# Window attention: the output projection's second block, the transposes' copies and the last projection piece placed differently

## The chip, the cores and the metric

The kernel runs on one core of one Trainium2 chip, in float32. The metric is the device time of one launch in microseconds. Before the change it is 5811.65 us, the median of three runs (5798.19 to 5814.1).

## The reference

The input x has shape (8, 56, 56, 192). Four layers follow one another; each normalises its input in groups and adds its result to it: two token-mixing layers with Toeplitz convolutions, a 7x7 depthwise convolution with an MLP, and a shifted-window attention. The change is in the last one, which computes this:

```python
x = jnp.roll(x, (-DISP, -DISP), (1, 2))       # DISP = 3, windows of WS*WS = 49
q, k, v = x @ Wq, x @ Wk, x @ Wv              # reshaped to (b, 6, nw, 49, 32)
scores = jnp.einsum('bhnqd,bhnkd->bhnqk', q, k) * DIM_V ** 0.5 + bias
...
attn = jax.nn.softmax(scores, axis=-1)
out = jnp.einsum('bhnqk,bhnkd->bhnqd', attn, v).reshape(b, n_h, n_w, -1)
out = jnp.roll(out @ Wfc + bfc, (DISP, DISP), (1, 2))
```

The reshape to (b, 6, nw, 49, 32) is one of memory order, without a transposition: a head is a stretch of rows, and its windows are runs of 49 times 32 numbers in it. Rows of the mask are added to some of the windows.

## The kernel before

The first three layers end at about 4900 us of the span; the attention takes the rest. It is one generator, `attention`, whose first steps are woven into the end of the MLP. The loop at its end, `for n in range(len(units) + 1)`, is what the change touches.

**Units, groups, slots.** A unit is half of one sample's rows, so there are 16, and one more turn of the loop that finishes the last. A unit's 48 windows per quarter are worked off in NG = 3 groups (`g` = 0, 1, 2; "first", "middle", "third" below). A group has four slots, `give(0)` to `give(3)`, at which pieces of other work are issued between the softmax's own. `order[g][slot]` lists them: 0 is a piece of the next unit's projection, 1 a block of the previous unit's output projection.

**Projection of the next unit** (`project`): ten pieces. Four value pieces (matmuls of L1176 and L1186, a copy on ScalarE, stores to a DRAM buffer and reloads by SP in another layout), then six query and key pieces (L1229), each with two copies into the tile `f`: one on VectorE (L1244) and one on ScalarE (L1242). The first group issues the four value pieces, the middle group two query pieces (slots 0 and 3), the third group the other four, the last of them in slot 3. The first scores of the next unit read what that last piece's copies write.

**Output projection of the previous unit** (`out`): two blocks. Block k0 covers 128 of the 192 output channels (48 matmuls, L1345), block k1 the remaining 64 (96 smaller ones). A block takes two PSUM tiles, and eight additions on VectorE (L1356) bring its result into the raw tiles `ra` (k0) or `rb` (k1). After k1, SP stores both to the output (L1366). k0 is issued in slot 1 of the middle group and k1 in slot 2. At the end of that group SP reloads the same two tiles (three buffers each) with the input of unit n+2 (L1133, L1135), and at the end of the third group `normalize` (L1151 on VectorE, L1159 on ScalarE) turns them into `xa` and `xb`, which have one buffer each and feed the next projection.

**Softmax.** In slot 0 and slot 1 of each group: `scores` (64 matmuls, L1259; on VectorE scaling with bias, L1271, and the maximum, L1280; on GpSimd the subtraction, L1281; on ScalarE the exponential, L1282), then after the slot's pieces `divide` (on VectorE the sum, L1289, and the reciprocal, L1290; on GpSimd the product, L1291). What a group has computed is used one group later: `turned` transposes it on TensorE (eight matmuls, L1297) and copies it from PSUM into `et`, for slot 0 by VectorE (L1307) and for slot 1 by ScalarE (L1305). `weighted` multiplies it with the values (64 matmuls, L1319), slot 0's ahead of `give(2)`, slot 1's after it, and `sixths` copies the result out (L1329 on VectorE, L1334 on ScalarE).

**PSUM** is one pool of four tiles, each two banks: `self.bank2 = lambda: ps.tile([128, 2, 512], F32, name="bank2")` with `bufs=4`. A piece of the projection, scores, transposes and a weighted sum take one tile each, a block of the output projection two.

**Order on the engines.** Each engine works off its own instructions in a fixed order, set when the program is built. It follows the order of the code, except that an instruction that can start sooner may stand ahead of another engine's result: in the trace the copy of L1307 runs between L1289 and L1290 in the middle and third groups, and the additions of k0 run behind the second sum, although the code has them ahead of it. On TensorE the order in the loop is that of the code.

Of the kernel before, what the change touches and what calls it, by code (L numbers as in the profile page):

```python
# [43 lines left out]
class Net:  # L44
# [1013 lines left out]
    def attention(self, L, xs, gn3, gnd, ys, vd):  # L1058
# [14 lines left out]
        if True:  # L1073
# [4 lines left out]
            def load_gr(i):  # L1078
                for half in HALF:
                    nc.sync.dma_start(gr[i][half], gnd[i].rearrange("(b c) s -> c b s", c=C)[128:C])  # L1080
# [169 lines left out]
            def scores(hh, g, i, qf, kf):  # L1250


                s = bank2()
                for n in range(8):
                    for half in range(2):
                        for c in range(2):
                            qd = slice(32 * (i + 2 * c), 32 * (i + 2 * c) + 32)
                            u = (16 * g + 8 * half + n) * WR
                            nc.tensor.matmul(  # L1259
                                s[64 * half : 64 * half + 64, c, n * WR : (n + 1) * WR],  # L1260
                                qf[qd, u : u + 64],
                                kf[qd, u : u + WR],
                                start=True,
                                stop=True,
                            )
                var = {0: 1, 3: 2}.get((2 * i + 3 * hh + g) % 4, 0)
                e = ering[count[0] % NE]
                count[0] += 1
                ev = e[:, :, :, :WR]
                e3 = e.rearrange("p c n k -> p (c n) k")[:, :, :WR]  # L1270
                nc.vector.scalar_tensor_tensor(  # L1271
                    ev,
                    view(s, 0, [[512, 2], [WR, 8], [1, WR]]),
                    math.sqrt(32.0),
                    view(bias, var * 8 * WR, [[0, 2], [WR, 8], [1, WR]]),
                    ALU.mult,
                    ALU.add,
                )
                mx = p.tile([128, 16], F32, name="mx", bufs=6)
                nc.vector.tensor_reduce(mx, e3, AX.X, ALU.max)  # L1280
                nc.gpsimd.tensor_sub(e3, e3, view(mx, 0, [[1, 16], [0, WR]]))  # L1281
                nc.scalar.activation(e3, e3, AF.Exp)  # L1282
                return e

            def divide(e):

                e3 = e.rearrange("p c n k -> p (c n) k")[:, :, :WR]
                sm = p.tile([128, 16], F32, name="sm", bufs=6)
                nc.vector.tensor_reduce(sm, e3, AX.X, ALU.add)  # L1289
                nc.vector.reciprocal(sm, sm)  # L1290
                nc.gpsimd.tensor_mul(e3, e3, view(sm, 0, [[1, 16], [0, WR]]))  # L1291

            def turned(e, i):
                pt = bank2()
                for c in range(2):
                    for m in range(4):
                        nc.tensor.transpose(  # L1297
                            pt[:113, c, m * 128 : m * 128 + 113],
                            e.rearrange("p c n k -> p c (n k)")[:113, c, m * 128 : m * 128 + 113],
                            self.ident[:113, :113],  # L1300
                        )
                et = self.at2.tile([113, 8, 113], F32, name="et", bufs=3)
                ev = pt.rearrange("p c (m q) -> p (c m) q", q=128)[:113, :, :113]
                if i:
                    nc.scalar.copy(et, ev)  # L1305
                else:
                    nc.vector.tensor_copy(et, ev)  # L1307
                return et
# [29 lines left out]
            def out(b, hh, ra, rb, oj):  # L1338
                for k, raw, n in ((0, ra, 7), (1, rb, 4)):
                    fs = [bank2(), bank2()]  # L1340
                    for j in range(6):
                        for i in range(4):
                            qd = slice(32 * i, 32 * i + 32)
                            for h in range(k + 1):
                                nc.tensor.matmul(  # L1345
                                    fs[i // 2][HALF[h] if k else slice(0, 128), i % 2, : n * W],
                                    wfc[qd, j, 128 * k : 128 * k + 128 - 64 * k],
                                    oj[qd, j, h * MT : h * MT + n * W],
                                    start=j == 0,
                                    stop=j == 5,  # L1350
                                )
                    for i in range(4):

                        for c, m, c2 in ((0, 53, 3), (53, 3, 0)):
                            to = raw[:, i, :, c2 : c2 + m]
                            nc.vector.scalar_tensor_tensor(  # L1356
                                to,
                                view(fs[i // 2], i % 2 * 512 + c, [[W, n], [1, m]]),
                                bfc[:, k : k + 1],
                                to,  # L1360
                                ALU.add,
                                ALU.add,
                            )
                    if k == 0:
                        yield
                rows(b, hh, ra, rb, (ys, lambda t, d: nc.sync.dma_start(d, t)), 1)  # L1366

            def step(gen):

                try:  # L1370
                    next(gen)
                except StopIteration as end:
                    return end.value
                return None
# [20 lines left out]
            late = None  # L1395


            order = (((0,), (0,), (0,), (0,)), ((0,), (1,), (1,), (0,)), ((0,), (0,), (0,), (0,)))
            for n in range(len(units) + 1):
                if n < len(units):  # L1400
                    (b, hh), (v, qf, kf) = units[n], now
                gen = project(*units[n + 1]) if n + 1 < len(units) else None
                outs = None
                now = None
                for g in range(NG):
                    if g == 1 and n:
                        outs = out(*units[n - 1], *raws.pop(n - 1), oj)

                    def give(at):
                        got = now  # L1410
                        for kind in order[g][at]:
                            if kind and outs is not None:
                                step(outs)
                            elif not kind and gen is not None:
                                got = step(gen)
                        return got

                    es, ets = [], []
                    for i in range(2):
                        if n < len(units):  # L1420
                            es.append(scores(hh, g, i, qf, kf))
                        now = give(i)
                        self.norm_part()
                        if n < len(units):
                            divide(es[i])
                        if late is not None:
                            ets.append(turned(late[1][i], i))
                    if late is not None:
                        g_late, es_late, v_late = late
                        if g_late == 0:  # L1430
                            ot = self.at2.tile([128, HR], F32, name="ot", bufs=1)
                            oj = self.at2.tile([128, 6, HT], F32, name="oj", bufs=1)
                        po = bank2()
                        weighted(g_late, 0, ets[0], v_late, po)
                    now = give(2)
                    if late is not None:
                        weighted(g_late, 1, ets[1], v_late, po)
                        sixths(g_late, po, ot, oj)
                    now = give(3)
                    late = (g, es, v) if es else None  # L1440
                    if g == 0 and n + 3 == len(units) // 2:
                        for more in self.all_norms():
                            pass
                        load_gr(1)
                    if g == 1 and n + 2 < len(units):
                        raws[n + 2] = load(*units[n + 2])
                    if g == 2 and n + 2 < len(units):
                        normalize(units[n + 2][0], *raws[n + 2])
# [197 lines left out]
```

## Time and profile before

| | |
|---|---|
| median of three runs | 5811.65 us |
| the profiled execution | 5810.6 us |
| its span, first to last instruction | 5808.7 us |
| mean granted TensorE clock | 0.957 |
| TensorE busy in the span | 5366.0 us (92%) |
| VectorE, ScalarE, GpSimd busy | 2367.7, 2262.1, 2205.1 us (41, 39, 38%) |
| attention loop, units 1 to 14 | 4951.82 to 5748.13 us |
| TensorE, VectorE busy in it | 715.51, 468.16 us of 796.31 |
| DMA engines in it, mean | 43%, 88 GB/s |

How it is read: a group of instructions is named by its line, engine and tiles. A wait is the idle time of an engine just before an instruction, put down to what released it; only waits of the engine that sets the pace cost time. "issue" is idle time for which the profile shows no releaser. The granted clock is the share of TensorE's full speed that the throttle allowed in a stretch. Matmuls overlap, so what one set of them costs is read from the start of one to the start of the next.

### The profile page before, as it was taken

The numbers are of one execution on the slowest core, as the hardware profiler recorded it, in microseconds if no ns is written. First come the engines' busy times: TensorE is split into PE (matmuls) and PEld (weight loads), VectorE is DVE, ScalarE is ACT, GpSimd is POOL, SyncE is SP. The second block draws the span as 40 slices with busy tenths as digits, with TensorE's granted clock in tenths as the row PEclk, the third lists the DMA queues.
The fourth block names the chain that finished last, engine by engine and source line by source line (L and its number), as shares of the span: only waits on it lengthen the run. The fifth ranks groups of instructions, "written<-read, shape, count | busy, mean of one in ns | idle before, by whom it ended". The sixth has DMA issues, their size and how long they took to land.

```text
span 5808.7 us, 144259 instructions
## 1 busy us (share of the span) xinstructions
PE 5366.0 (92%) x64672; PEld 3891.7 (67%) x64672; DVE 2367.7 (41%) x3770; ACT 2262.1 (39%) x2990; POOL 2205.1 (38%) x1528
## 2 busy tenths in 40 slices
PE   6998887999999999998888889989999999889898
PEld 3776665777777777776666678856664445666666
DVE  6444544233553333552333322332213232565655
ACT  2434444443554444554444322242323333333332
POOL 2335566564665566565566200000001001333333
PEclk9999998999999999999999899999999999999998
DMA  8559997888886887878998566634444223344442
GB/s 277 137 151 263 273 291 210 266 253 231 239 257 200 243 249 252 238 233 225 293 307 268 169 216 223 217 117 159 148 160 117 67 62 58 80 95 85 90 87 62
DMA packets 1029770, 1098.79 MB, mean 189 GB/s; under 512 B 232768, under 2 KB 966976, under 8 KB 1013728
## 3 DMA queue, kind: packets, MB, share of 16 engines
q1 hardware_dynamic: 993568, 888.57, 56.2%
q0 software_dynamic: 35584, 200.99, 9.0%
q8 instruction: 509, 8.34, 0.6%
q14 instruction: 109, 0.89, 0.0%
HBM read 725.48 MB, written 363.94 MB: 188 GB/s over the span
## 4 chain that ended last, share of the span: by engine, by line
PE 54%; POOL 7%; DMA 7%; SPq 6%; DVE 5%; issue 3%; ACT 3%; POOLq 0%; DVEq 0%; ACTq 0%
PE bank L263 8%; PE bank L955 6%; PE bank L816 5%; PE bank L1035 4%; PE bank L530 4%; PE bank L575 4%; SPq L392 3%; PE bank L405 3%; POOL s L427 3%; PE bank L1049 3%; DMA t<-L_sum 2%; SPq L379 2%; PE bank L539 2%; PE bank L1229 2%; DMA qv<-t 2%
## 5 line engine op out<-in xcount | busy, mean ns | idle before, releaser
L263 PE MATMUL bank<-wq,t 128*128 128x256 f32 (+4 forms) x7680 | 1300.3, 377 | 84.0 <-DVE t L272 46.2
L263 PEld LDWEIGHTS bank<-wq,t 128*128 128x128 f32 (+2 forms) x7680 | 1013.8, 192 | 364.7 <-issue 103.7
L272 DVE TENSOR_TENSOR t<-bank,wq 128x1024 f32<-128x1024 f32 (+3 forms) x480 | 517.7, 1112 | 773.7 <-PE bank L263 551.6
L304 POOL TENSOR_TENSOR t<-t 128x1024 f32<-128x1024 f32 (+2 forms) x288 | 518.9, 1815 | 654.3 <-ACT t L301 342.1
L412 ACT COPY ot<-bank 128x896 f32<-128x896 f32 x576 | 493.0, 914 | 631.3 <-PE bank L405 357.8
L427 POOL TENSOR_TENSOR s<-s,ot 128x1568 f32<-128x1568 f32 x144 | 618.6, 4300 | 68.7 <-DVE ot L425 68.2
L405 PE MATMUL bank<-q,tm 56*32 56x224 f32 x18432 | 522.2, 363 | 78.0 <-DMA tm<-L_tab 25.9
L301 ACT ACTIVATE t<-t 128x2048 f32<-128x2048 f32 (+2 forms) x288 | 422.0, 1488 | 397.2 <-DVE t L272 388.7
L405 PEld LDWEIGHTS bank<-q,tm 56*32 56x32 f32 x18432 | 351.1, 108 | 216.3 <-issue 108.5
L556 POOL TENSOR_TENSOR t<-t,t 128x896 f32<-128x896 f32 x168 | 347.2, 2085 | 362.8 <-DMA t<-L_sum 185.2
L588 DVE SCALAR_TENSOR_TENSOR t<-bank,wo,t 128x448 f32<-128x448 f32 x112 | 76.5, 683 | 889.9 <-ACT t L584 492.3
L530 PE MATMUL bank<-t,wo 128*128 128x224 f32 x1792 | 395.9, 377 | 45.5 <-ACT t L509 22.4
L955 PE MATMUL bank<-z,w 128*128 128x448 f32 (+1 forms) x1344 | 416.0, 557 | 3.1 <-ACT h L964 3.1
L549 ACT ACTIVATE t<-bank,wo 128x448 f32<-128x448 f32 x448 | 248.0, 635 | 406.7 <-PE bank L539 377.0
L530 PEld LDWEIGHTS bank<-t,wo 128*128 128x128 f32 x1792 | 351.7, 202 | 81.6 <-issue 30.8
L575 PE MATMUL bank<-t,wo 128*128 128x224 f32 x1792 | 378.9, 366 | 0.0
L127 POOL DMA_DIRECT2D x<-x x64 | 36.7, 573 | 865.4 <-DVE x L986 836.2
L575 PEld LDWEIGHTS bank<-t,wo 128*128 128x128 f32 x1792 | 338.0, 194 | 34.2 <-issue 32.4
L816 PEld LDWEIGHTS bank<-xt,cm 113*112 113x112 f32 x3072 | 315.0, 180 | 43.7 <-issue 38.3
L423 DVE STREAM_TRANSPOSE s<-ot 128x1792 f32<-128x1792 f32 x144 | 292.7, 2035 | 115.5 <-DMA L_sum<-s 86.6
L816 PE MATMUL bank<-xt,cm 113*112 113x108 f32 (+2 forms) x3072 | 326.2, 266 | 6.4 <-issue 3.3
L955 PEld LDWEIGHTS bank<-z,w 128*128 128x128 f32 (+1 forms) x1344 | 183.3, 190 | 208.2 <-issue 199.2
(149 smaller groups left out, 6996.6 us busy)
## 6 DMA issues: line engine op xcount, KB each, us to landing
q<-qv SPq DMA_DIRECT2D x36, 3584.0 KB
q<-qv SPq DMA_DIRECT2D x72, 1568.0 KB
L_sum<-s POOLq DMA_DIRECT2D x288, 392.0 KB, 7.7
t<-L_sum SPq DMA_DIRECT2D x112, 1008.0 KB
qv<-t SPq DMA_DIRECT2D x192, 512.0 KB
cm<-in_L_cm SPq DMA_DIRECT2D x96, 896.0 KB
tm<-L_tab SPq DMA_DIRECT2D x288, 240.0 KB
x<-t POOLq DMA_DIRECT2D x112, 336.0 KB, 7.1
```

Source lines behind the costliest of these rows:

```text
L263: nc.tensor.matmul(pp[:m, b, 256 * j : 256 * j + k], x[rows, j, 2 if part else b, s : s + m], w[rows, part, c0 + c : c0 + c + k],  start=p ...
L272: nc.vector.tensor_add(z[:m, c : c + k, :], view(pp[:m], 0, [[1, k], [256, 4]]), view(bias[:m], c0 + c, [[1, k], [0, 4]]),)
L301: nc.scalar.activation(z[:m, :n, :], z[:m, :n, :], AF.Silu)
L304: nc.gpsimd.tensor_mul(prod[:m, :k], half[:, :, 0], half[:, :, 1])
L405: nc.tensor.matmul(pt[32 * j : 32 * j + 32, r, hf * 224 : (hf + 1) * 224], tm[rows, at : at + 32], q[rows, :, 4 * c : 4 * c + 4], start=Tr ...
L412: nc.scalar.copy(view(ot, 4 * (g % 4), [[16, 2], [32, 112], [1, 4]]), view(pt, 0, [[512, 2], [4, 112], [1, 4]]),)
L427: nc.gpsimd.tensor_add(to, to, view(of, 0, [[1, 28], [32, 56]]))
L530: mm(gs[c // 2][:, b, c % 2 * 256 : c % 2 * 256 + N], pw[:, 0, 128 * c : 128 * c + 128], xn[:, b], start=c % 2 == 0, stop=False,)
L556: gate.tensor_mul(to, to, pg)
L575: mm(P[:, b, :N], ow[:, c, 0:128], g[:, 4 * b + c], start=False, stop=c == 3 and b == 1)
L816: nc.tensor.matmul(pc[:, 128 * e + 4 * m0 : 128 * e + 4 * m1], cm[:113, e, k, :], xt[:, m0 - 1 + k : m1 - 1 + k, c + e, :], start=n == 0 a ...
L955: nc.tensor.matmul(phs[c][:, s, :TT], w0[rows, part, at : at + 128], z[rows, Z[2 if part else s], :], start=part == flip, stop=part != flip,)
```

## The change

Three edits in `attention`, in 15 lines:

```diff
                 et = self.at2.tile([113, 8, 113], F32, name="et", bufs=3)
                 ev = pt.rearrange("p c (m q) -> p (c m) q", q=128)[:113, :, :113]
-                if i:
+                if i == 0:
                     nc.scalar.copy(et, ev)
                 else:
                     nc.vector.tensor_copy(et, ev)
...
-            order = (((0,), (0,), (0,), (0,)), ((0,), (1,), (1,), (0,)), ((0,), (0,), (0,), (0,)))
+            order = (((0,), (0,), (0,), (0,)), ((0,), (1, 0), (0,), (1,)), ((0,), (0,), (0,), ()))
...
                         now = give(i)
                         self.norm_part()
+                        if late is not None:
+                            ets.append(turned(late[1][i], i))
                         if n < len(units):
                             divide(es[i])
-                        if late is not None:
-                            ets.append(turned(late[1][i], i))
```

In the middle group, slot 1 now issues k0 and then a query piece, slot 2 a query piece, and slot 3 k1; so the middle group has three pieces of the projection instead of two. The third group has three instead of four, the last of them in slot 2, ahead of the second weighted sum; its slot 3 is empty. The stores of k1, which are issued with it, and the reload after it move with it on SP. Slot 0's transposes are copied by ScalarE and slot 1's by VectorE. In both slots the transposes and their copy are issued ahead of the division of the current group's scores.

## The prediction

> **What bounds the kernel now.** Only the attention loop is touched, so I read the granted clock first, then the busy time by stretch, TensorE's waits in the loop, and the instructions of one unit in order of time. The steady part is units 1 to 14: from the first scores of unit 1 (4951.82) to those of unit 15 (5748.13), 796.31 us or 56.88 a unit. What TensorE waited for there, in total, times, longest:
>
> ```profile
> PE bank L1345 <- DVE ra L1356: 40.1, 14, 2.9
> PE bank L1319 <- ACT et L1305: 16.3, 23, 1.2
> PE bank L1259 <- DVE f L1244: 14.5, 15, 1.1
> ```
>
> TensorE is busy for 715.51 of the 796.31 us, VectorE for 468.16, ScalarE 267.15, GpSimd 256.12. So TensorE sets the pace, and time is to be had in its waits. The first is once a unit, always 2.85 to 2.89: the second output-projection block (k1) waits for a PSUM bank of the first (k0), which VectorE's adds free. One unit shows why:
>
> ```profile
> 5313.84 4.97 PE L1345 MATMUL bank<-oj,wfc 32*128 32x392 f32 x48
> ...
> 5318.37 1.52 POOL L1281 TENSOR_TENSOR e<-e,mx 128x784 f32<-128x784 f32 x1 [0.34 <-DVE mx L1280]
> ...
> 5319.92 0.87 ACT L1282 ACTIVATE e<-e 128x784 f32<-128x784 f32 x1 [5.39 <-POOL e L1281]
> ...
> 5320.83 0.97 DVE L1289 TENSOR_REDUCE sm<-e 128x16 f32<-128x784 f32 x1 [2.62 <-ACT e L1282]
> 5321.83 0.25 DVE L1290 RECIPROCAL sm<-sm 128x16 f32<-128x16 f32 x1
> 5322.00 2.67 DVE L1356 SCALAR_TENSOR_TENSOR ra<-bank,bfc,ra 128x371 f32<-128x371 f32 x8
> ...
> 5323.50 4.79 PE L1345 MATMUL bank<-oj,wfc 32*64 32x224 f32 x96 [2.89 <-DVE ra L1356]
> ```
>
> k0 ends at 5318.74, but its adds stand on VectorE behind the second softmax's sum (L1289), which waits for GpSimd's subtraction and ScalarE's exponential. k1 starts after four of the eight adds. It then pays twice, because the clock falls (columns: stretch, length, busy time of five engines, granted clock, DMA share, GB/s):
>
> ```profile
> 5308.34:5323.50 15.16, 12.28 (x322) 8.65 (x321) 9.15 (x15) 3.99 (x6) 5.83 (x4) 0.98 0.72 79
> 5323.50:5332.03 8.53, 8.53 (x224) 6.19 (x224) 4.08 (x13) 0.72 (x1) 0.24 (x1) 0.64 0.30 105
> ```
>
> The same stretch of all 14 units (9.86 us from the wait's start) has a clock of 0.83 in 11 and 0.65 in 3. Start to start at full clock: scores 1.08, a value piece 2.32, a query/key piece 2.36, transposes 0.98, weighted sum 0.84, k0 4.90; k1 takes 2.51 in unit 15, where it doesn't wait (5770.55 to 5773.06). From the middle group's second scores to the third group's first that adds to 1.08+4.90+0.98+0.84+2.51+0.84+2.36 = 13.51; the 14 units take 18.26 on average. The loss of 4.75 is 2.86 of waiting and 1.89 of slow clock.
>
> **The change, part by part.** I lay one unit out anew with these durations, zero at the first scores of the middle group (5308.34 in the unit above). Profiled groups last 16.09, 22.67 and 18.12 on average (sum 56.88).
>
> *Transposes' copies.* The first goes from VectorE (mean 1093 ns) to ScalarE (899), the second the other way, and both are issued before that slot's division. In the first group, the second copy now sits on ScalarE behind the second exponential, and the weighted sum waits 0.73 on average (10.2 us over 14). On VectorE it can start when the transposes end, 8.8 after the group's scores, and end by 10.0; the weighted sum wants it at 11.9, and the sum that could hold it up isn't ready before 11.9. So the wait goes: **-0.73**. The bounds: 0 to -0.73. On ScalarE the other copy, at worst ahead of the exponential, delays it by 0.4; TensorE asks for neither for several us, and ScalarE idles over 3 us there, so I cost it at nothing. Without that cover it would be 0.9.
>
> *k1 last in its group.* The middle group gets one query piece more (2.36) and the third one less, so compare with 22.67+2.36 = 25.03. Without waits it would be 4.42+13.51+2.36 = 20.29. New order on TensorE: k0 to 10.40, piece to 12.76, transposes to 13.74, weighted sum, piece, weighted sum, k1. VectorE: with the first transposes' copy gone, the second scores' chain (bias, max, GpSimd 1.52, exp 0.87, sum) ends 0.4 to 0.9 sooner, so k0's adds begin at 12.8 to 13.3 instead of 13.66. There are four PSUM tiles: at 13.74 k0 holds two, the piece and the transposes one each, and the weighted sum needs one. The first comes free after four adds (1.35), 14.2 to 14.8: a wait of 0.45 to 1.05. The next piece takes k0's other tile after all eight adds, some 0.5 later still. The f copy (0.62) and the second transposes' copy (1.09) end at 17.2 to 17.7, before the second weighted sum (18.0 to 18.5); k1 then finds free tiles. The third group starts at 21.3 to 21.8; I take 21.5: **-3.5**. Bounds: 20.29 (-4.74) and, if the weighted sum gets its tile only after the piece's f copy behind all adds and both transposes' copy, w0 at 18.3, a wait of 4.55 and a slow clock again: 20.29+4.55+1.4 = 26.2 (+1.2).
>
> *Its DMAs.* k1's adds, the stores of rb and the reload of ra and rb for unit n+2 move one slot later on SP, which has nothing else queued until the next unit's value pieces. In the unit shown k1 ends at 5328.22 and the DMA engines fall quiet at about 5340.3, 12.1 later. ScalarE wants rb at about 13.3 after k1 at the earliest, and TensorE wants its result at 18. Cost nothing; a reload over 4.7 us later would cost each further us in full.
>
> *Last projection piece a slot sooner.* The weighted sum (0.84) now covers part of the unit's closing wait. That wait today:
>
> ```profile
> 5347.98 0.96 PE L1229 MATMUL bank<-xb,Wk 64*32 64x224 f32 x32
> 5348.12 1.28 DVE L1151 TENSOR_SCALAR xa<-ra,gn 128x1484 f32<-128x1484 f32 x2 [0.49 <-PE bank L1229]
> 5349.32 0.62 DVE L1244 COPY f<-bank 128x448 f32<-128x448 f32 x1
> 5349.99 1.15 PE L1259 MATMUL bank<-f,f 32*64 32x49 f32 x64 [1.05 <-DVE f L1244]
> ```
>
> The normalisation stands ahead of the f copy that the next scores need. In the new third group TensorE's own work is 12.88 (two scores, three pieces, two transposes, two weighted sums). But its softmax chain starts later: k1's adds (2.03) now stand before its first bias. Its last sum ended 13.5 after the group's start before; I get 13.4 to 13.9, the reciprocal 13.65 to 14.15, normalisation (1.29) to 15.2, f copy to 15.8. The next scores start at 15.6 to 16.1, say 15.85, against 18.12-2.36 = 15.76: **+0.1**. So a stall of 3.0 stands where 1.05 stood: that is what is late next. With the f copy before the normalisation it would be 14.55 (-1.2); with both before the sum 13.2 (-2.6); with the weighted sum's copy (0.97) also ahead 16.8 (+1.1).
>
> *The clock after that stall.* Today's closing waits of 1.05 leave the clock at 1.00; those of 2.86 always bring it down. A wait of 2.7 to 3.2 is nearest the latter: **+1.4**, k1's extra in units with 0.83 (3.9 against 2.51). Bounds: 0 and 1.9.
>
> The Trainium skill, "TensorE: Matmul & The Clock Gate", section "What's actually happening", puts the drop after at least one idle window of about 3.4 us; this trace shows it after 2.86. By that rule the stall would cost no clock and the sum would be 57 us.
>
> **Sum.** -0.73-3.5+0.1+1.4 = -2.73 a unit, 14 units: -38 us. Units 0, 15 and 16 lack k1's wait; nothing is taken for them. The profiled execution is 5810.6 (span 5808.7 and 1.9 around it), so 5772; the median of the runs is 1 us above it: **5773**. Its own range: no clock loss (-57) to 1.9 and the wider ends (-20), 5755 to 5792.
>
> **Rivals.** *(A) The closing stall doesn't grow*, since the f copy is ahead of the normalisation: for it, the normalisation needs a reload that is now only just there; against it, all units before have it first. 0.73+3.5+1.2 = 5.4 a unit, -76: 5736.
>
> *(B) The second transposes' copy queues behind the sum on VectorE*, one wait for another: in the first group the sum ends at 12.9, the copy at 14.0, and the weighted sum waits 2.1 instead of 0.73. Then -2.73+0.73+1.4 = -0.6 a unit, -8: 5803. For it, VectorE's order isn't the code's (the reciprocal runs after the transposes' copy in the middle group); against it, the code now issues the copy first.
>
> *(C) Slower: the wait moves to the weighted sum's PSUM tile*, the bound of 26.2 above, on top of the closing stall: -0.73+1.2+0.1+1.4 = +2.0 a unit, +28: 5840. It decides against the change from a wait of some 2.6 us there. For it: all four tiles are then held. Against: before, k1 got its tile after just four adds.
>
> **Chances.** Forecast 0.45, A 0.27, B 0.13, C 0.15. A difference under 0.3% (17 us) can't be told from none. Faster: the forecast, A and a little of B, 0.75; same: most of B, 0.12; slower: C, 0.13. Range: down to A with some spare, 5725; up to B, 5806.
>
> **What would show it.** Right: no wait of L1345 for L1356; L1319's for ScalarE gone in the first groups; waits of about 0.5 to 1 before the weighted sum and piece after k0; the wait of L1259 for the f copy at 2.7 to 3.2 with a clock near 0.8 after it; unit 54.1. Wrong: L1319 or L1229 waiting over 2 us for L1356 or L1307 (B, C), or L1259's wait still near 1 (A). A late reload would show as the normalisation waiting for a DMA.

## The result and the profile after

The changed kernel takes 5817.16 us, the median of 20 runs (5803.95 to 5828.85), against 5804.59 for 20 runs of the kernel before (5798.19 to 5825.58): a ratio of 1.0019 with a 95% interval of 1.0011 to 1.0027. By the bound of 0.3% that is no change, if anything a small loss; 38 us of gain were forecast. (The forecast counted them from 5811.65, the median of three runs, which lies 7 above that of the 20.) The profiled execution takes 5819.75 us, its span is 5818.0 with a mean granted clock of 0.956.

The span grew by 9.3 us. Units 1 to 14 now reach from 4955.50 to 5750.45: 794.95 us, 1.4 less than before. Ahead of them unit 0 takes 53.91 instead of 50.81 (+3.1) and starts 0.6 later; behind them, from unit 15's first scores to the end, stand 67.55 instead of 60.57 (+7.0). So there are two losses to explain, a gain that did not come in the loop and a new cost at its end. What TensorE waits for in the loop, in the profile after (total, times, longest):

```profile
PE bank L1259 <- DVE f L1244: 29.5, 14, 2.2
PE bank L1319 <- DVE et L1307: 16.7, 13, 2.0
PE bank L1259 <- issue: 8.8, 13, 1.2
PE bank L1319 <- PE bank L1297: 5.9, 14, 0.5
PE bank L1345 <- issue: 5.1, 8, 1.2
PE bank L1229 <- DVE ra L1356: 4.8, 14, 0.3
```

The wait of k1 for k0's additions (40.1 us before) is gone, and with it the weighted sums' wait for ScalarE's copy: 16.3 before, of which 10.2 in the 14 first groups and 6.0 in nine of the third ones. In their place the next unit's scores wait 29.5 instead of 14.5 for the f copy, and the third groups' weighted sum waits 16.7 for a transposes' copy that is now VectorE's. The middle group itself went as laid out. Unit 7 of the changed kernel, TensorE's instructions in order of time; its middle group starts at 5314.37:

```profile
5319.86 4.97 PE L1345 MATMUL bank<-oj,wfc 32*128 32x392 f32 x48
...
5328.64 1.02 PE L1319 MATMUL bank<-et,v 49*32 49x49 f32 x64 [0.46 <-PE bank L1297]
5330.00 1.53 PE L1229 MATMUL bank<-xa,Wq 128*32 128x224 f32 x32 [0.34 <-DVE ra L1356]
...
5333.11 0.63 PE L1345 MATMUL bank<-oj,wfc 32*64 32x224 f32 x15
```

k0's additions begin at 5327.17. Four of them, 1.34 at 2.68 for eight, end at 5328.51, and the weighted sum starts 0.13 later: its 0.46 is the wait for a PSUM tile, although the row names the transposes, which had ended. (That follows from the times; a1 below has the same distance with later additions.) The piece behind it waits 0.34 for the rest. k1 runs without waiting for VectorE, and the third group starts 21.69 after the middle one.

The third group is where it is lost. Its end in the same unit, all engines:

```profile
5349.06 0.97 DVE L1289 TENSOR_REDUCE sm<-e 128x16 f32<-128x784 f32 x1 [2.09 <-ACT e L1282]
...
5349.95 1.09 DVE L1307 COPY et<-bank 113x904 f32<-113x904 f32 x1
5350.95 0.24 DVE L1290 RECIPROCAL sm<-sm 128x16 f32<-128x16 f32 x1
...
5351.09 0.90 PE L1319 MATMUL bank<-et,v 49*32 49x49 f32 x64 [1.52 <-DVE et L1307]
5351.11 2.39 DVE L1151 TENSOR_SCALAR xa<-ra,gn 128x1484 f32<-128x1484 f32 x2
5351.34 2.10 POOL L1291 TENSOR_TENSOR e<-e,sm 128x784 f32<-128x784 f32 x1 [3.22 <-DVE sm L1290]
5353.42 0.61 DVE L1244 COPY f<-bank 128x448 f32<-128x448 f32 x1
...
5354.18 1.96 PE L1259 MATMUL bank<-f,f 32*64 32x49 f32 x64 [2.19 <-DVE f L1244]
```

VectorE works off one chain: the sum, then the second transposes' copy, for which the weighted sum waits (1.52), then the reciprocal, then the normalisation, which takes 2.39 here and 1.28 before, and only then the f copy, for which the next scores wait (2.19). The normalisation runs beside GpSimd's product, which itself takes 2.10 instead of 1.52. Before the change the two followed one another, and the weighted sum of this unit already waited, for ScalarE's copy (the normalisation of that unit, at 5348.12, is shown in the prediction):

```profile
5345.68 0.90 PE L1319 MATMUL bank<-et,v 49*32 49x49 f32 x64 [1.16 <-ACT et L1305]
...
5345.93 1.53 POOL L1291 TENSOR_TENSOR e<-e,sm 128x784 f32<-128x784 f32 x1 [2.34 <-DVE sm L1290]
```

And the clock is low after the closing wait of the changed kernel. The stretches of 9.19 us from the start of that wait, at the ends of units 2 and 7 (columns as in the prediction):

```profile
5069.35:5078.54 9.19, 8.14 (x171) 7.00 (x172) 5.95 (x10) 5.07 (x7) 2.40 (x2) 1.00 0.14 36
5351.99:5361.18 9.19, 7.00 (x89) 6.04 (x88) 4.87 (x6) 3.07 (x5) 2.97 (x2) 0.63 0.02 4
```

At the end of unit 2 the weighted sum did not wait for its copy and the scores waited 1.05: clock 1.00. At the 13 other ends of units 0 to 13 the scores waited 2.19, and the clock was 0.63 or 0.64 in nine and 0.81 in four.

Averages over units 1 to 14, from the first scores of a group to those of the next:

| us | first group | middle | third | unit |
|---|---|---|---|---|
| before | 16.09 | 22.67 | 18.12 | 56.88 |
| forecast | 16.76 | 21.5 | 15.85 | 54.1 |
| after | 17.32 | 21.84 | 17.62 | 56.78 |

In some units of the changed kernel the first few scores of the third group run among the last matmuls of k1, so the border between middle and third group is sure to 0.1 only: by the very first of these scores the two are 21.72 and 17.74. The same goes for the kernels below that issue k1 last.

### The profile page after: what moved, and what is told of

It reads as the page before. It is cut to its first block, busy times and chain, and to the rows that moved or that the text cites. A ratio compares the mean times of both kernels' runs of the same rounds, so it can differ in the third digit from the quotient of the medians.

```text
span 5818.0 us, 144285 instructions
## 1 busy us (share of the span) xinstructions
PE 5374.7 (92%) x64672; PEld 3910.2 (67%) x64672; DVE 2386.2 (41%) x3770; ACT 2266.6 (39%) x2990; POOL 2214.8 (38%) x1528
## 4 chain that ended last, share of the span: by engine, by line
PE 55%; POOL 7%; DVE 7%; DMA 6%; SPq 5%; issue 3%; ACT 2%; POOLq 0%; DVEq 0%; ACTq 0%
PE bank L263 8%; PE bank L955 6%; PE bank L816 5%; PE bank L530 5%; PE bank L1035 4%; PE bank L575 4%; PE bank L405 3%; SPq L392 3%; PE bank L1049 3%; POOL s L427 3%; PE bank L539 2%; PE bank L578 2%; SPq L379 2%; PE bank L1176 2%; DMA t<-L_sum 2%
## 5 line engine op out<-in xcount | busy, mean ns | idle before, releaser
L530 PEld LDWEIGHTS bank<-t,wo 128*128 128x128 f32 x1792 | 352.6, 203 | 84.3 <-issue 30.4
```

The lines of the kernel that those rows point to most:

```text
L530: mm(gs[c // 2][:, b, c % 2 * 256 : c % 2 * 256 + N], pw[:, 0, 128 * c : 128 * c + 128], xn[:, b], start=c % 2 == 0, stop=False,)
```

## The experiments

Two readings stood against each other. One: the gain is there and VectorE's queue at the end of the unit takes it back; a kernel with the f copy out of that queue must be faster. The other: the new order itself costs what it gives, by k1 late, a piece missing as cover, or copies on the wrong engine; then one of the parts alone must be better than the whole. Ratios are to the kernel before on the same chip (medians 5804.59 for "after", 5807.94 for a1 to a5, 5802.92 for a6 to a9, 5804.03 for b1 to b4). Groups, unit and tail (from unit 15's first scores to the end) come from each kernel's one profile.

| kernel | median us | ratio (95%) | first, middle, third | unit | tail |
|---|---|---|---|---|---|
| before | | 1 | 16.09, 22.67, 18.12 | 56.88 | 60.6 |
| after | 5817.16 | 1.0019 (1.0011 to 1.0027) | 17.32, 21.84, 17.62 | 56.78 | 67.6 |
| a1 order only | 5829.33 | 1.0035 (1.002 to 1.0049) | 17.71, 22.93, 17.44 | 58.07 | 62.8 |
| a2 copies only | 5806.36 | 0.9999 (0.999 to 1.0009) | 15.06, 23.03, 18.13 | 56.22 | 67.4 |
| a4 f copy on ScalarE | 5782.24 | 0.996 (0.9945 to 0.9975) | 17.63, 21.77, 15.47 | 54.88 | 69.3 |
| a5 copy ahead of sum | 5792.9 | 0.9978 (0.9968 to 0.9987) | 16.68, 21.76, 16.82 | 55.26 | 66.3 |
| a6 = a4 + a5 | 5763.81 | 0.9932 (0.9911 to 0.9953) | 17.48, 21.63, 14.16 | 53.27 | 68.5 |
| a7 late division | 5757.78 | 0.9921 (0.9903 to 0.9939) | 15.83, 21.83, 15.50 | 53.15 | 66.6 |
| a8 = a7 + a4 | 5739.91 | 0.989 (0.9873 to 0.9906) | 15.49, 21.94, 14.27 | 51.70 | 68.0 |
| a9 product on VectorE | 5814.32 | one run | 17.51, 21.89, 17.51 | 56.91 | 67.4 |
| b1 = a8, k1 early | 5791.98 | 0.9982 (0.9969 to 0.9995) | 15.17, 22.98, 17.74 | 55.89 | 67.2 |
| b2 = a8, old copies at the end | 5728.32 | 0.9868 (0.9853 to 0.9882) | 15.49, 21.67, 14.26 | 51.42 | 61.2 |
| b3 = a8, last piece in slot 3 | 5755.57 | 0.9915 (0.99 to 0.9929) | 15.06, 21.91, 16.19 | 53.16 | 68.5 |
| b4 = a8, old copies | 5780.7 | 0.9957 (0.9943 to 0.9971) | 16.71, 22.92, 15.45 | 55.08 | 63.1 |

**The parts alone.** a1 keeps the new order of the pieces and undoes the copies and the place of the division:

```diff
-                if i == 0:
+                if i:
                     nc.scalar.copy(et, ev)
...
-                        if late is not None:
-                            ets.append(turned(late[1][i], i))
                         if n < len(units):
                             divide(es[i])
+                        if late is not None:
+                            ets.append(turned(late[1][i], i))
```

> Only the new order of the pieces (k1 last, last projection piece in slot 2); the transposes' copies stay on their old engines and the division ahead of them. Theory, read off the changed kernel's trace: k1's wait of 2.86 and its slow clock go (middle group with one piece more about 22, against 25.0 before), but the third group gives it back, as the next unit's scores now wait over 2 us for the f copy, which stands behind the softmax's last sum and the normalisation, and the clock falls after that. The first groups keep their 0.73 wait for ScalarE's copy. So 5815 to 5830, no better than the whole change. Rival (the copies' swap is what spoils the change): clearly faster, about 5770.

a2 keeps those and undoes the order:

```diff
-            order = (((0,), (0,), (0,), (0,)), ((0,), (1, 0), (0,), (1,)), ((0,), (0,), (0,), ()))
+            order = (((0,), (0,), (0,), (0,)), ((0,), (1,), (1,), (0,)), ((0,), (0,), (0,), (0,)))
```

> Only the swap of the transposes' copies and their place ahead of the division; the order of the pieces as before. Theory: first groups lose their 0.73 wait, k0's additions begin 0.4 to 0.9 sooner and shorten k1's wait to about 2, the third group's second copy now stands behind the sum on VectorE and makes the weighted sum wait some 0.5 to 1 longer than before: -0.9 a unit, about 5792 against 5805 before. Rival (the swap is what spoils the change): slower than before, 5815 or more.

The order alone loses (1.0035): the scores' wait for the f copy is there without the copies' change (29.0 us over 14), and the weighted sum waits for ScalarE's copy in 27 places (23.2). In each middle group its first weighted sum also waits 1.3 where the changed kernel has 0.4, in rows that name no releaser; in one unit k0's additions begin at 5335.05 and this sum at 5336.51, 0.12 after the fourth of them, so by the times it is the wait for the PSUM tile again, longer because the first transposes' copy is back on VectorE ahead of the chain. The copies alone are worth 0.66 a unit, 9 us, by the first group (15.06 against 16.09, the predicted kind of gain and more), and lose 6.8 at the end; in sum nothing (0.9999), where 5792 was expected. k1's wait shrinks less than expected, from 40.1 to 35.7 us in all, and the middle group is not shorter (23.03 against 22.67). So the copies' change is what makes the new order bearable in the loop, and the new cost at the end belongs to it: tails of 67.4 here, 62.8 with the order alone. (The clock does not tell these tails apart: its mean is 0.69 here, 0.73 in a1, 0.74 in the changed kernel.)

**The queue at the end of the unit.** a4 takes the last piece's f copy off VectorE:

```diff
-                            if th:
+                            if th or (m, j0) == (1, 4):
                                 nc.scalar.copy(to, of)
```

> The changed kernel, with the f copy of a unit's last projection piece on ScalarE in place of VectorE (448 columns, some 0.5 us there). Theory (the gain is given back at the unit's end, by the scores' wait for a f copy that stands behind the sum, the transposes' copy and the normalisation): the wait of 2.19 of L1259 goes, the clock stays at 1.00 in the first group, a shorter wait moves to the value piece, which needs the normalisation; -2 to -3.4 a unit, 5770 to 5790. Rival (the third group is bound by its softmax chain, whatever stands behind it; the f copy only shows as the last releaser): within 5 us of the changed kernel's 5817.

a5 makes the second transposes' copy of the third group run ahead of the sum (`put` holds that copy):

```diff
-                        if n < len(units):
+                        if n < len(units) and late is not None and g == 2 and i:
+                            with tc.issue_after(put[-1].ins):
+                                divide(es[i])
+                        elif n < len(units):
                             divide(es[i])
```

> The changed kernel, with one pair exchanged on VectorE: in the third group the copy of the second transposes stands ahead of the second sum instead of behind it. Theory: the weighted sum's wait of 1.5 goes, but the sum, the normalisation and the f copy move only 0.8 sooner, so the scores' wait grows to about 3 and the slow clock stays: -0.8 a unit, about 5805. Rival (the weighted sum's wait is what was given back): -1.5 a unit or more, 5796 or less.

a6 is both edits together.

> The last two edits together: in the third group the transposes' copy ahead of the sum, and the f copy of the last piece on ScalarE. Theory: neither the weighted sum nor the scores wait at the unit's end any more; the value piece waits about 1.2 for the normalisation and up to 1.6 for the second half of it. If a wait under 1.2 leaves the clock alone the first group's slow clock goes as well: -3.5 to -5 a unit against the changed kernel, 5745 to 5768. Rival (the group is bound by its softmax chain): no better than the better of the two, 5780.

a4 takes 2.15 off the third group (15.47 against 17.62), and the closing wait is gone. Its first group stays at 17.63, with the clock at 0.63 in the 8 us from 5329.68, although TensorE waited only once, 1.54 us, for the transposes' copy. a5 removes that wait instead, and the closing one grows (35.1 over 14, up to 3.1): one long stall for two shorter ones, 5793. That is the figure of a5's rival, not of its theory (5805): the third group fell by the 0.8 expected, but the first one, where the slow clock was to stay, by another 0.6. Both together bring the third group to 14.16, but now the next value pieces wait for the normalised input itself: L1176 for VectorE 11.1 us in 10 places, L1186 for ScalarE 11.5 in 11, and the first group is at 17.48. The normalisation cannot simply be put last.

a7 leaves the normalisation where it is and moves what stood ahead of it: the division of the third group's second scores, whose result is wanted a group later, is issued behind the normalisation (`normalize` returns its last VectorE instruction):

```diff
-                        if n < len(units):
+                        if n < len(units) and not (g == 2 and i and n + 2 < len(units)):
                             divide(es[i])
...
-                        normalize(units[n + 2][0], *raws[n + 2])
+                        with tc.issue_after(normalize(units[n + 2][0], *raws[n + 2])):
+                            divide(es[1])
```

> The changed kernel with one thing moved: in the third group the second division (sum, reciprocal, GpSimd's product) is issued after the normalisation of unit n+2 and queued behind it on VectorE. Theory: the transposes' copy, the normalisation and the f copy no longer stand behind the sum, and the normalisation no longer runs beside GpSimd's product, so its second part takes 0.32 instead of 1.42; the closing waits of 1.5 and 2.2 shrink to some 0.3, and with them the slow clock in the first group goes. A unit of about 51.5 against 56.8, 5745. Rival (the division is needed early): the next unit's transposes wait for GpSimd's product, 5800 or more.

a8 is a7 with a4's line.

> The kernel before it in this list, with the f copy of the last piece on ScalarE as well. Theory: nothing of weight is left for the f copy to wait for, so 0 to -0.3 a unit, 5740 to 5745. Rival: if the f copy still stood behind the normalisation at a cost, -1 a unit or more.

VectorE at the end of a unit in a7:

```profile
5322.82 1.29 DVE L1151 TENSOR_SCALAR xa<-ra,gn 128x1484 f32<-128x1484 f32 x2 [0.79 <-PE bank L1230]
5324.02 0.96 DVE L1290 TENSOR_REDUCE sm<-e 128x16 f32<-128x784 f32 x1
5324.90 0.61 DVE L1245 COPY f<-bank 128x448 f32<-128x448 f32 x1
```

(Its lines are one further on: L1290 is the sum, L1245 the f copy.) The normalisation starts as soon as the last piece is through with its input, and is back at 1.29, since GpSimd's product comes later. The transposes' copy is done before it. The unit falls to 53.15, in the third group and, with the clock, in the first. It does not reach the 51.5 expected, since the scores still wait for the f copy, now behind the normalisation and the sum: 12.9 us in 14 places (up to 1.3). So a8, which takes the f copy out as well, gains 1.45 a unit more, the figure of its rival and not the 0 to 0.3 of its theory, and reaches 51.70, and 5739.91 us. That is better than the forecast of 54.1, because the stall that the forecast accepted is gone too.

a9 tests the collision by itself. The product of the third group's second scores goes to VectorE, and nothing else changes:

```diff
-            def divide(e):
+            def divide(e, by=nc.gpsimd):
...
-                            divide(es[i])
+                            divide(es[i], nc.vector if g == 2 and i else nc.gpsimd)
```

> The changed kernel with the third group's second product (784 columns) on VectorE instead of GpSimd. Theory (VectorE's normalisation and GpSimd's product slow each other when they run side by side): the normalisation's pair takes 1.3 instead of 2.39, its second part 0.32 instead of 1.42; the product's own 0.9 takes the place of that, so the time stays within 10 us of the changed kernel. Rival (the second part is slow for another reason, as its place behind the reciprocal): the pair stays at 2.4.

VectorE at the end of a unit in a9:

```profile
5343.80 0.98 DVE L1291 TENSOR_TENSOR e<-e,sm 128x784 f32<-128x784 f32 x1
5344.69 1.28 DVE L1151 TENSOR_SCALAR xa<-ra,gn 128x1484 f32<-128x1484 f32 x2
5345.89 0.62 DVE L1244 COPY f<-bank 128x448 f32<-128x448 f32 x1
```

With GpSimd idle the normalisation takes 1.28 again; its smaller part, 84 columns, takes 319 ns, against a mean of 1423 in the changed kernel. The product's 0.98 on VectorE takes the place of the 1.1 so freed, and unit (56.91) and time (5814.32, one run) stay. a9 alone leaves the place behind the reciprocal as a rival cause, as both are gone in it. b4 (below) speaks against it: one normalisation there, behind an f copy and not a reciprocal, starts 0.56 into GpSimd's subtraction and takes 1.98, where those beside nothing take 1.29:

```profile
5492.19 1.52 POOL L1282 TENSOR_TENSOR e<-e,mx 128x784 f32<-128x784 f32 x1 [0.31 <-DVE mx L1281]
...
5492.75 1.98 DVE L1151 TENSOR_SCALAR xa<-ra,gn 128x1484 f32<-128x1484 f32 x2 [0.18 <-PE bank L1230]
```

So the collision is real and costs 1.1 a unit in the changed kernel, and it is the length of the chain ahead of the f copy, whatever it consists of, that sets the third group.

**What each part of the change is worth once that queue is mended.** b1 is a8 with the old order of the pieces (a2's line), b3 is a8 with the third group's last piece back in slot 3:

```diff
-            order = (((0,), (0,), (0,), (0,)), ((0,), (1, 0), (0,), (1,)), ((0,), (0,), (0,), ()))
+            order = (((0,), (0,), (0,), (0,)), ((0,), (1, 0), (0,), (1,)), ((), (0,), (0,), (0,)))
```

> The best kernel so far (late division and the f copy on ScalarE, 5740) with the order of the pieces as before the change: k1 in slot 2 behind k0, two pieces in the middle group, four in the third. Theory (k1's move is worth its 3.5 us a unit, hidden by the loss at the unit's end): k1 waits about 2 for k0's additions again, the clock falls after it, the middle group takes 23.0 with one piece less: +3 a unit, about 5782. Rival (only the unit's end matters): 5750 or less.

> The best kernel so far, with the third group's three pieces in slots 1, 2 and 3 instead of 0, 1 and 2: k1 stays last, but the unit's last projection piece ends the unit again. Theory: nothing covers the f copy and the normalisation any more, so the next scores and value piece wait about 1 longer: +1 a unit, about 5754. Rival (the last piece sooner is what put it into the softmax's way): faster than 5735.

b4 is a8 with the old copies and the division's old place (a1's edit; the late division of a7 stays), b2 has these only from unit 15 on, where no later unit follows. Its line for the copies (the transposes move behind the division under the same condition):

```diff
-                if i == 0:
+                if (i == 0) == (n + 1 < len(units)):
                     nc.scalar.copy(et, ev)
```

> The best kernel so far, with the transposes' copies on their old engines and behind the division, everything else kept. Theory: the first groups' weighted sum waits 0.5 to 0.75 again and the first copy on VectorE puts the middle group's chain 0.5 to 1 back: +1 to +1.5 a unit, against 5 to 7 less at the end: about 5750. Rival (the swap costs more than it brings): 5735 or less.

> The best kernel so far, with the copies of the transposes on their old engines and behind the division from unit 15 on, where no unit is projected any more. Theory: from unit 15's first scores to the end the kernels with the swapped copies take 66 to 69 us, the ones without 60.6 and 62.8, since there the softmax's own chain sets the pace and VectorE is its busiest engine: the old engines give 5 to 7 back, 5734. Rival (the longer tail is the clock's phase): no difference.

With k1 early again (b1) its wait is back, now in two pieces:

```profile
PE bank L1346 <- DVE ra L1357: 36.5, 28, 2.0
```

and the unit is 55.89, so the new order is worth 4.19 a unit, or some 53 us of the whole by the ratios (0.9982 against 0.989), more than the 3 expected. The last piece a slot sooner is worth 1.46 a unit (b3: 53.16; the scores wait 12.8 us in 15 places for ScalarE's f copy). The new copies and the division's place are worth 3.4 a unit in the loop, more than I had put on them (b4: 55.08; the weighted sum waits 26.6 us in 27 places for ScalarE, and 1.3 in each middle group for its tile, as in a1) and cost 4.9 at the end (68.0 against 63.1). Why they cost something there, the changed kernel's own end shows, VectorE in order of time:

```profile
5769.92 0.97 DVE L1289 TENSOR_REDUCE sm<-e 128x16 f32<-128x784 f32 x1 [1.46 <-ACT e L1282]
...
5771.68 2.73 DVE L1356 SCALAR_TENSOR_TENSOR ra<-bank,bfc,ra 128x371 f32<-128x371 f32 x8 [0.51 <-PE bank L1345]
5774.32 1.09 DVE L1307 COPY et<-bank 113x904 f32<-113x904 f32 x1
```

The second transposes' copy stands behind all eight additions of k0, TensorE waits 1.51 for it, and k1 and the third group's scores stand behind that weighted sum. k1 then runs at a clock of 0.64 and takes some 4.6 us, against 2.51 at 1.00 before. In the loop a projection piece lies in between; unit 15 has none. The third group's scores start 30.4 after unit 15's first, 25.8 before the change. b2 has the old copies there and the new ones in the loop. Its loop and its tail:

```profile
4944.37:5664.27 719.90, 688.16 (x19712) 532.03 (x19712) 461.28 (x742) 277.87 (x351) 256.54 (x182) 1.00 0.46 97
5664.27:5725.50 61.23, 44.42 (x1256) 35.16 (x1248) 35.92 (x65) 16.92 (x15) 19.02 (x13) 0.80 0.14 42
```

The clock is 1.00 over the whole loop, TensorE is busy for 688.16 of 719.90 us, the tail is 61.23, and the kernel takes 5728.32 us: a ratio of 0.9868 (0.9853 to 0.9882), faster than both the kernel before and the changed one.

## Why the prediction was wrong

**k1 last in its group** held. Middle group 21.84 against 22.67+2.36 = 25.03 is -3.2 for a forecast of -3.5. In the unit shown k0 ends 10.4 after the group's start, its additions begin at 12.80, the weighted sum starts at 14.27 and the third group at 21.69, each within the forecast's ranges. b1 prices the new order at 4.19 a unit with the rest mended. The PSUM wait of rival C, 4.55 at its bound, came as 0.46. *Its DMAs* cost nothing: no row shows the normalisation waiting for a reload.

**Transposes' copies**: the first group's wait for ScalarE went, as -0.73 said; a2 measures -1.03 for that group. Putting the first copy on ScalarE cost nothing in the loop, as said. But the step followed the second copy on VectorE in the first group only (and the next step in the middle one); in the third it was not followed at all, although the weighted sum there already waited 6.0 us in nine units for ScalarE's copy. What the step said of k0's additions, 0.4 to 0.9 sooner without the first copy on VectorE, held: they begin 12.80 after the group's start in the unit shown and 13.67 after it in that of a1, and the weighted sum waits 0.4 for its tile instead of 1.3.

**Last projection piece a slot sooner** is the step that failed. It took the next scores to start at 15.85 in the third group; the mean is 17.62. Its sum came almost when it said (13.4 to 13.9, and 13.97 in the unit shown). But the reciprocal was put right behind the sum, and the transposes' copy, 1.0, came between; and the normalisation was put at 1.29 because it took 1.28 before, where GpSimd's product was already over (5345.93+1.53 = 5347.46, ahead of 5348.12). In the changed kernel the product, released by the reciprocal just ahead, runs in the same microseconds: 2.39, or 1.1 more. 1.0+1.1 = 2.1 of the 2.27 by which the scores of the unit shown came later than 15.85 (18.12). The rest is a sum that ends just past the late edge of its range. a4 shows that the scores hang on this chain (-2.15 in the third group with the f copy out of it), a9 the second part by itself.

The first part is rival B's mechanism, the copy queued behind the sum, but in another place. B was thought of for the first group, where it did not happen, and its price of -0.6 a unit came near the measured -0.10 without its mechanism there. The forecast had even listed the cases "with both before the sum" and "with the weighted sum's copy (0.97) also ahead", without asking for the transposes' copy. Against B it held that the code issues the copy first. The queue does not follow the code there: in unit 7 the transposes end at 5346.38, and VectorE stands idle for 2.09 ahead of the sum with the copy behind it. Why the build orders them so stays open; a5 shows that the copy can stand ahead.

The Trainium skill, "SBUF — State Buffer", section "Who interferes with whom", says that a tensor_scalar on VectorE can hold a port pair that GpSimd also needs, and that the later of the two waits until the first is done. The trace agrees in kind: 319 ns alone, a mean of 1423 beside the product, and the product 2.10 instead of 1.52; in the unit shown the two end within 0.06 of each other. That this instruction holds the pair no run here shows by itself. Before the change the two never met in the loop (mean 319 ns), so no wait told of it; what told of it is that the reorder brings them together.

**The clock after that stall** was right in kind and sized too small: +1.4 forecast; the first group came out 0.56 longer than the 16.76 that follow from it, so 1.96 if all of it is the clock, just above the upper bound of 1.9. The stall was to be one of 2.7 to 3.2; in the unit shown it was two, 1.52 and 2.19. The step also read the profile before too simply: not all closing waits of 1.05 left the clock at 1.00, two (1.03 and 1.06) went with 0.81.

**Units 0, 15 and 16**, for which nothing was taken because they lack k1's wait (which rules out a gain there, not a cost), cost 10.7 (0.6 and 3.1 ahead, 7.0 behind). Ahead, unit 0 ends with a closing wait of 2.19 where 1.05 stood, and TensorE is busy for 47.12 of it instead of 44.74, at a clock of 0.87 instead of 0.90; where in unit 0 that clock is lost was not followed. The 3.1 is of one profile each and not shown to be the change's: unit 0 takes 51.26 in a9, whose loop is as long as the changed kernel's, and 45.4 to 52.6 in the other runs. Behind, it is the copies, as a1, a2, b2 and b4 show.

Together: the unit missed by 56.78-54.1 = 2.7, of which 1.77 in the third group, 0.56 in the first and 0.34 in the middle; 37 us over 14 units. With the 10.7 outside the loop that is 48 by these two profiles, and 5819.75 stands 48 above the 5772 of the sum.

Three small slips of the forecast bear on nothing: k1's wait was 2.84 to 2.89, the sum without a loss of clock is 57.8 and not 57, and 16.8 against 15.76 is +1.0 and not +1.1.

Left open: TensorE's "issue" gaps in the loop, for which no releaser shows, are 10.6 us before, 19.2 after and 18.7 in b2. They were not tried. In the unit shown one of 1.20 splits the third group's first scores, and VectorE waits 0.40 for them, which is part of why its sum ends late. That the 0.34 of the middle group are such gaps (the one ahead of k1 above all, 5.1 us over 8) is argued, not shown.

## What to carry to other kernels

When a move takes the cover from a wait, lay out the queue of the engine that ends that wait instruction by instruction, with every instruction that the change puts on it, and ask of each long one whether its result is wanted there; here a division whose result nobody needed before the next group was worth some 57 us (a7 against after, 0.9921 against 1.0019 of the kernel before). A duration from a profile holds for the neighbours it had: an instruction that is moved beside work of GpSimd has to be priced anew. And a change tuned for the steady loop should be read in the last turn too, where the work that covered it is missing.

## What the runs showed of the hardware

- **The clock falls after shorter waits than the profile before let one think.** Waits of 2.86 brought it down there; of the 15 closing waits of 0.7 to 1.06, 13 left it at 0.99 or 1.00 in the 9.19 us from their start, and two went with 0.81. In a4 the scores no longer wait for the f copy, so the weighted sum's wait comes alone or ahead of short ones of the value pieces (0.2 to 0.6 in ten places, 1.24 in five). After ten such waits of 1.35 to 1.71 the clock was 0.64 to 0.81 nine times, after four of up to 1.24 it was 1.00 three times. In three units no other wait lies in the 9.19 us: 1.54, 1.54 and 1.71, with 0.64, 0.65 and 0.65. The first of these, over 8 us:

```profile
5329.68:5337.68 8.00, 7.00 (x145) 5.84 (x145) 6.15 (x7) 3.44 (x5) 3.62 (x2) 0.63 0.02 5
```

  In the changed kernel the same wait of 2.19 gave 0.63 in nine units and 0.81 in four. In a7, closing waits of 0.37 to 1.27 went with 0.81 in six units and 1.00 in eight, without order by length. So above 1.35 the clock nearly always fell; below that the length of the wait does not tell, and what else decides was not tried. The section "What's actually happening" of the Trainium skill's "TensorE: Matmul & The Clock Gate" asks for at least one idle window of about 3.4 us; measured here is a fall after single waits of 1.54 and up.

- **A short VectorE instruction can cost over four times its own time beside GpSimd**: 84 columns 1423 ns on average against 319. The sums (L1289, 0.96 to 0.97) and the copies out of PSUM kept their times throughout.
